# Four attention layers on one core: 64-row products issued together, feed-forward in fours, context values moved between passes

## The chip, the core and the metric

The kernel runs on one core of a Trainium2 chip. The core has a matrix engine (TensorE, PE in the profile, with weight loads listed apart as PEld), a vector engine (VectorE, DVE), an activation engine (ScalarE, ACT), a general engine (GpSimd, POOL) and SyncE (SP), which here only issues transfers. TensorE writes to PSUM, which has eight banks of 512 float32 values in each of 128 partitions. The metric is the device time of one execution in microseconds; of several runs the median counts.

## What is computed

The input x has 8 batches of 256 tokens with 320 channels, the context 8 batches of 120 tokens with 192 channels. Four layers follow each other:

```python
# layer 0: quantised attention, 20 heads of 16
def attention(x, ctx, Wq, Wk, Wv, Wo, bo, heads):
    q, k, v = fq_sym(x @ Wq), fq_sym(ctx @ Wk), fq_sym(ctx @ Wv)   # 8 bits, one step for the whole tensor
    ...
    w = fq_zero(softmax(q @ k * dh ** -0.5))                       # again one step for the whole tensor
    return (w @ v) @ Wo + bo
x = x + attention(layer_norm(x), layer_norm(x), ...)
x = x + attention(layer_norm(x), ctx, ...)
x = x + geglu_ff(layer_norm(x))        # (h @ W1 + b1) in halves a, g; a * gelu(g) @ W2 + b2; 320 -> 2 x 1280 -> 320
# layer 1: the same three steps without quantisation, exact gelu
# layer 2: attention to 104 text tokens plus attention to 16 image tokens, one output projection
# layer 3: attention to 116 tokens, 8 heads of 40, and a second chain of two small attentions with 4 tokens
```

A quantisation step needs the maximum over a whole tensor. So each attention of layer 0 is done in two passes: one to find the largest weight, one to compute with it.

## The kernel before

**Products of 320 rows.** A matrix product on TensorE contracts over partitions, at most 128. 320 channels are 128 + 128 + 64 rows, and the 192 channels of the context 128 + 64. The last 64 rows are kept twice, in the lower and in the upper half of the partitions. Two outputs are computed side by side: `duo` (L122) issues the 128-row terms of both, then the 64-row term of one output in the lower half of the array and that of the other in the upper half. `by_weight` and `by_token` (L132, L138) choose the halves. In the profile the 128-row terms are L127 and the 64-row terms L129. Each float32 product is two matmul records.

**PSUM.** `pair` gives two adjoining banks out of a rotation of three (6 banks, tile `pf`), `bank` a single one out of two (tile `pa`). A tile comes free when the engine that empties it is done.

**Layer 0's self attention** is an object `Quant`, called `s`; cross attention is another, `c`. `project_all` (L1143) runs over the batches: values, then the next batch's transposes (`turn`), then queries, keys, and the third 128 columns of both. In the first pass scores and their maxima (L1332, L1335), exponentials (L1376, L1383) and sums (L1398) are woven together. `weight_steps` (L1424) ends it: the logarithm of all sums on ScalarE (L1428), the smallest sum through a transpose and back (`all_max`, L469), the step (L1441), its logarithm (L1442). The second pass `out_all` (L1457) starts with `shift` (L1446), five VectorE steps on the logarithms, whose result `nTs` enters the scores through L1376.

**Between them** stands work for cross attention. `keys_all` is woven into s's first pass, `queries_all` (L1204) into its second: normalising on GpSimd (L301), transposes (L314) three rounds later, projections from the sixth. `values_all` (L1193) makes the context's values, one batch a step: four records of TensorE (L120, `pf<-v,ctxT`), a ScalarE copy (L1200), a VectorE maximum (L1139). Three steps are woven into the end of s's second pass and five into c's first pass.

**Keys and values of later layers** (`context_steps`, L642) are woven into c's two passes and go to DRAM; their 128-row products are L668, the 64-row ones L670.

**Feed-forward** (`ff_item`, L545) works on 512 tokens at a time, four items a layer. For each of 10 blocks of 128 hidden channels it takes a pair, issues four 128-row products (L564: gate and value, two terms each), two 64-row products (L568), GELU on ScalarE (L572) and a multiply on VectorE (L573), and yields. Then come 40 products with the second weight (L120).

**Order.** `weave` runs several generators in turn, and `run_flow` (L609) does so for the items of layers 1 to 3: while one item is in its main part, the next finds its score maxima, the one after it projects, and the one before finishes its output projection. Inside the order so written, a scheduler of the framework places the instructions of each engine[...].

Of the kernel before, what the change touches and what calls it, by code (L numbers as in the profile page):

```python
# [18 lines left out]
P = 128  # L19
# [35 lines left out]
class Kernel:  # L55
# [66 lines left out]
    def duo(self, outs, terms):  # L122

        n = len(terms[0]) - 1
        for c in range(n):
            for o, t in zip(outs, terms):
                self.nc.tensor.matmul(o, *t[c], start=c == 0, stop=False)  # L127
        for o, t in zip(outs, terms):
            self.nc.tensor.matmul(o, *t[n], start=False, stop=True)  # L129
# [176 lines left out]
    def turned(self, x, dst, at, ln=None):  # L306


        nc = self.nc
        ps = self.pair()  # L310
        for i, n in CH:
            for t in range(TPB):
                o = i % 2 * N + t * P
                nc.tensor.transpose(ps[:n, i // 2, o : o + P], x[:, t, i * P : i * P + n], self.ident)  # L314
        if ln is None:
            nc.scalar.copy(dst[:, :2, at : at + N], ps[:, 0, :].rearrange("p (c n) -> p c n", c=2))
            for r in (0, 64):
                nc.scalar.copy(dst[r : r + 64, 2, at : at + N], ps[:64, 1, :N])
            return
        for i, r, n in ((0, 0, P), (1, 0, P), (2, 0, 64), (2, 64, 64)):  # L320
            g = COL_LN + 6 * ln + i
            nc.scalar.activation(
                dst[r : r + n, i, at : at + N], ps[:n, i // 2, i % 2 * N : (i % 2 + 1) * N], AF.Identity,
                bias=self.cols[r : r + n, g + 3 : g + 4], scale=self.cols[r : r + n, g : g + 1],
            )
# [156 lines left out]
    def heads_item(self, b, ln, w, brow, kind):  # L482
# [4 lines left out]
        def project():  # L487
# [30 lines left out]
            self.duo([ps[:, m, :N] for m in range(2)], two((w["q"], w["q"]), (0, 1), 2))  # L518
            yield
            self.duo([ps[:, 0, N:]], two((w["q"],), (2,), 1))  # L520
# [24 lines left out]
    def ff_item(self, blk, ln, which, func, w, brow):  # L545
# [11 lines left out]
        def out():  # L557
            xT = it["x"]
            hT = [self.hp.tile([P, 4, 512], F32, tag="big", name="hT", bufs=4) for _ in range(3)]
            for i in range(NF):  # L560
                s = self.pair()
                for k, col in ((1, (NF + i) * P), (0, i * P)):
                    for c in range(2):
                        nc.tensor.matmul(s[:, k, :], w1[:, c, col : col + P], xT[:, c, :], start=c == 0, stop=False)  # L564

                for k in (1, 0):
                    r = 64 * k
                    nc.tensor.matmul(  # L568
                        s[:, k, :], w1c[r : r + 64, i * P : (i + 1) * P], xT[r : r + 64, 2, :], start=False, stop=True
                    )  # L570
                gl = self.work.tile([P, TB], F32, tag="gl", name="gl")
                nc.scalar.activation(gl, s[:, 1, :], func, bias=self.cols[:, b1 + NF + i : b1 + NF + i + 1])  # L572
                nc.vector.scalar_tensor_tensor(  # L573
                    hT[i // 4][:, i % 4, :], s[:, 0, :], self.cols[:, b1 + i : b1 + i + 1], gl, ALU.add, ALU.mult
                )
                yield
# [65 lines left out]
    def context_steps(self):  # L642
# [22 lines left out]
        def both(outs, whole, halves):  # L665

            for i, o in enumerate(outs):
                nc.tensor.matmul(o, *whole[i], start=True, stop=False)  # L668
            for i, o in enumerate(outs):
                nc.tensor.matmul(o, *halves[i], start=False, stop=True)  # L670

        def keys_to(ps, w, cols, b, k0, k1):
# [3 lines left out]
            for o, gs in cols:  # L676
# [4 lines left out]
                    [(w[half(i), 1, s], self.ctxT[half(i), 1, b, k0:k1]) for i, s in enumerate(c)],  # L681
# [196 lines left out]
    def last_item(self, b, w, brow, to):  # L878
# [8 lines left out]
        def project():  # L887
# [31 lines left out]
            for r in range(2):  # L919
                self.duo(  # L920
                    [ps[:, i, r * N : (r + 1) * N] for i in range(2)],
                    [self.by_weight(w["wq"], xT, 2 * r + i, i) for i in range(2)],
                )
# [7 lines left out]
            for c, t in ((0, 0), (1, 0), (0, 1), (1, 1), (2, 0), (2, 1)):  # L931
# [4 lines left out]
                    bd[rows, c, :nh, :].rearrange("p h r -> p (h r)"), start=c == 0, stop=c == 2,  # L936
# [180 lines left out]
class Quant:  # L1117
# [25 lines left out]
    def project_all(self):  # L1143
# [4 lines left out]
        def turn(b):  # L1148
            xT = k.work.tile([P, 3, N], F32, tag="xT", name="xT")
            k.turned(x, xT, 0, self.ln)  # L1150
# [4 lines left out]
        for b in range(B):  # L1155
# [6 lines left out]
            ps = k.pair()  # L1162
            k.duo([ps[:, t, :C] for t in range(TPB)], [k.by_token(w["v"], xT, t, t) for t in range(TPB)])
            nc.scalar.copy(v, ps[:, :, :C])
            if b + 1 < B:
                after = turn(b + 1)
            qv, kv = (a.rearrange("p (c n) -> p c n", c=3) for a in (q, kt))
            pq, pk = k.pair(), k.pair()
            for ps, n in ((pq, "q"), (pk, "k")):
                k.duo([ps[:, m, :N] for m in range(2)], [k.by_weight(w[n], xT, m, m) for m in range(2)])  # L1170
            k.duo([pq[:, 0, N:], pk[:, 1, N:]], [k.by_weight(w[n], xT, 2, i) for i, n in enumerate("qk")])
# [32 lines left out]
    def queries_all(self):  # L1204
# [20 lines left out]
        for r in range(5 * B + 4):  # L1225
            for b in range(B):
                if r - 5 * b in todo:
                    todo[r - 5 * b](b)
# [300 lines left out]
def kernel(ctx: ExitStack, tc: tile.TileContext, a, out):  # L1529
    k = Kernel(ctx, tc, a, out)  # L1530
    with ExitStack() as es:
# [15 lines left out]
        with tc.tile_pool(name="l0", bufs=1) as pool:  # L1547
            k.open_quant(pool)
            with tc.tile_pool(name="l0_keys", bufs=1, side="right") as kpool:
# [9 lines left out]
                for b in range(B):  # L1559
                    c.top(1, b, c.kk[b])  # L1560
                s.weight_steps()
                v = c.values_all()
                k.weave((0, s.out_all()), (8, c.queries_all()), (5 * B + 4, islice(v, 3)))
# [9 lines left out]
            for _ in c.whole(0, True):  # L1573
# [3 lines left out]
                (0, c.tops_all()), (n + 4, c.sums_all()), (0, c.whole_all()), (5, v),  # L1577
# [122 lines left out]
```

## Time and profile before

| | |
|---|---|
| runs | 2265.03, 2272.55, 2274.88 us; median 2272.55 |
| profiled execution | 2260.05 us |
| its span | 2258.2 us |
| granted TensorE clock, mean | 0.971 |
| TensorE busy | 2078.1 us (92%) |
| VectorE, ScalarE, GpSimd busy | 1119.0, 824.4, 363.2 us |
| layer 0: projections; self attention; cross attention | 13 to 112; 118 to 417; 424 to 678 us |
| layer 0 feed-forward; layer 1 attention; its feed-forward | 678 to 988; 989 to 1470; 1470 to 1750 us |
| layers 2 and 3 | from 1750 us |

The span goes from the first to the last instruction of the profiled execution. A row of a group names line, engine, operation, output and inputs and, behind an x, the number of records. Ends of matmul records are modelled, so starts are the surer quantity. The granted clock is the share of full speed that TensorE was allowed in a stretch.

### The profile page before, as it was taken

The numbers are of one execution on the slowest core, as the hardware profiler recorded it, in microseconds if no ns is written. First come the engines' busy times: TensorE is split into PE (matmuls) and PEld (weight loads), VectorE is DVE, ScalarE is ACT, GpSimd is POOL, SyncE is SP. The second block draws the span as 40 slices with busy tenths as digits, with TensorE's granted clock in tenths as the row PEclk, the third lists the DMA queues.
The fourth block names the chain that finished last, engine by engine and source line by source line (L and its number), as shares of the span: only waits on it lengthen the run. The fifth ranks groups of instructions, "written<-read, shape, count | busy, mean of one in ns | idle before, by whom it ended". The sixth has DMA issues, their size and how long they took to land.

```text
span 2258.2 us, 38244 instructions
## 1 busy us (share of the span) xinstructions
PE 2078.1 (92%) x16413; PEld 1177.0 (52%) x16413; DVE 1119.0 (50%) x1693; ACT 824.4 (37%) x1249; POOL 363.2 (16%) x368
## 2 busy tenths in 40 slices
PE   7978888898889999999999999899999799999997
PEld 4643345544444455465555555444455455566664
DVE  4288677444861221235555566611121566556465
ACT  2337878467542121124444443401201333222221
POOL 1093056620520000000000001100000100000100
PEclk9979889899899999999999999999999899999999
DMA  4010000542120000020000010100000201000000
GB/s 115 10 18 2 2 1 2 149 119 61 49 88 3 1 0 1 1 91 2 2 2 21 27 35 24 47 0 0 1 1 1 68 25 33 11 24 24 23 16 19
DMA packets 79304, 63.23 MB, mean 28 GB/s; under 512 B 48410, under 2 KB 68318, under 8 KB 78622
## 3 DMA queue, kind: packets, MB, share of 16 engines
q1 hardware_dynamic: 75070, 57.06, 9.0%
q10 hardware_dynamic: 4064, 3.71, 0.6%
q8 instruction: 130, 2.13, 0.4%
q14 instruction: 40, 0.33, 0.0%
HBM read 42.61 MB, written 17.37 MB: 27 GB/s over the span
## 4 chain that ended last, share of the span: by engine, by line
PE 74%; DVE 15%; ACT 4%; issue 2%; SPq 2%; DMA 1%; POOL 1%; ACTq 0%; DVEq 0%; POOLq 0%
PE pf L564 13%; PE pf L120 12%; PE pf L127 9%; PE pa L120 6%; PE pa L431 6%; PE pf L414 4%; PE pf L568 4%; PE pf L129 3%; DVE negm L1335 3%; PE pf L1376 3%; DVE rs L439 2%; PE pf L369 2%; PE pa L1398 2%; DVE negm L376 2%; DVE rs L1054 2%
## 5 line engine op out<-in xcount | busy, mean ns | idle before, releaser
L564 PE MATMUL pf<-xTf,ff 128*128 128x512 f32 x640 | 294.8, 603 | 3.5 <-DVE negm L376 2.5
L420 ACT ACTIVATE e<-pf 128x1024 f32<-128x1024 f32 (+2 forms) x176 | 157.7, 944 | 223.6 <-PE pf L414 216.8
L376 DVE TENSOR_REDUCE negm<-pf 128x4 f32<-128x1024 f32 (+4 forms) x224 | 187.8, 885 | 93.2 <-PE pf L369 93.2
L439 DVE RECIPROCAL rs<-pa 128x256 f32<-128x256 f32 x88 | 152.3, 1746 | 147.3 <-PE pa L431 147.3
L573 DVE SCALAR_TENSOR_TENSOR hT<-pf,cols_sb,gl 128x512 f32<-128x512 f32 x80 | 60.0, 750 | 331.2 <-ACT gl L572 331.2
L564 PEld LDWEIGHTS pf<-xTf,ff 128*128 128x128 f32 x640 | 115.1, 190 | 161.6 <-issue 154.9
L461 POOL TENSOR_TENSOR xb<-x_sb,brow 128x640 f32<-128x640 f32 x40 | 62.2, 1554 | 797.5 <-DVE x_sb L467 754.1
L1383 ACT ACTIVATE e<-pf,sc_s 128x1024 f32<-128x1024 f32 x160 | 169.6, 1117 | 50.8 <-PE pf L1376 44.7
L1335 DVE TENSOR_REDUCE negm<-pf 128x4 f32<-128x1024 f32 (+2 forms) x128 | 143.4, 1139 | 70.0 <-PE pf L1332 63.3
L120 PE MATMUL pf<-ff,hT 128*128 128x320 f32 x640 | 174.4, 434 | 0.0
L572 ACT ACTIVATE gl<-pf,cols_sb 128x512 f32<-128x512 f32 x80 | 55.0, 687 | 304.9 <-PE pf L568 304.9
L120 PEld LDWEIGHTS pf<-ff,hT 128*128 128x128 f32 x640 | 120.9, 190 | 55.5 <-issue 6.1
L414 PE MATMUL pf<-qT,kT 32*128 32x256 f32 (+1 forms) x1280 | 128.3, 411 | 19.3 <-DMA qT<-nT 11.0
L369 PE MATMUL pf<-kT,qT 32*128 32x120 f32 (+1 forms) x1920 | 112.7, 328 | 18.3 <-ACT e L420 18.3
L120 PE MATMUL pa<-o,oT 128*128 128x320 f32 x352 | 105.7, 442 | 12.8 <-DVE oT L440 11.6
L581 POOL TENSOR_TENSOR xb<-x_sb,brow 128x640 f32<-128x640 f32 x16 | 25.2, 1573 | 559.5 <-DVE x_sb L586 543.6
L369 PEld LDWEIGHTS pf<-kT,qT 32*128 32x128 f32 x1920 | 83.4, 189 | 55.4 <-ACT e L420 28.4
L1376 PE MATMUL pf<-Q,K 32*128 32x256 bf16 (+1 forms) x960 | 89.3, 294 | 24.9 <-DVE negm L1335 14.6
L431 PE MATMUL pa<-e,v 128*32 128x256 f32 (+1 forms) x1280 | 106.4, 389 | 2.3 <-ACT e L420 1.7
L414 PEld LDWEIGHTS pf<-qT,kT 32*128 32x128 f32 (+1 forms) x1280 | 72.2, 182 | 66.9 <-issue 34.6
L1491 DVE TENSOR_SCALAR w<-e 128x1024 bf16<-128x1024 f32 (+2 forms) x128 | 87.4, 691 | 37.4 <-ACT e L1383 36.4
L127 PE MATMUL pf<-xT,q 128*128 128x256 f32 x384 | 101.9, 394 | 2.1 <-DVE hT L573 1.9
(279 smaller groups left out, 3357.0 us busy)
## 6 DMA issues: line engine op xcount, KB each, us to landing
ff<-in_L_xattn_Wff_dram SPq DMA_DIRECT2D x1, 2560.0 KB
qT<-nT SPq DMA_DIRECT2D x160, 4.0 KB
ff<-in_L_xattn_ff_w_dram SPq DMA_DIRECT2D x1, 2560.0 KB
out_dram<-x_sb SPq DMA_DIRECT2D x16, 160.0 KB
kd_cross<-kst SPq DMA_DIRECT2D x8, 300.0 KB
vd_cross<-vst SPq DMA_DIRECT2D x8, 300.0 KB
vd_both<-vst SPq DMA_DIRECT2D x8, 300.0 KB
kT<-kd_cross SPq DMA_DIRECT2D x8, 300.0 KB
```

The costliest lines, as they stand in the source:

```text
L120: self.nc.tensor.matmul(out, l, r, start=i == 0, stop=i == len(pairs) - 1)
L127: self.nc.tensor.matmul(o, *t[c], start=c == 0, stop=False)
L369: nc.tensor.matmul(s[j // 2][:, j % 2, o : o + nk], qT[r : r + PAD, g, t * P : (t + 1) * P], kT[r : r + PAD, g, :nk], start=True, stop=True,)
L376: nc.vector.tensor_reduce(negm[:, n, 2 * i : 2 * i + 2, g0 : g0 + len(gs), :].rearrange("p j g t -> p j (g t)"), sv[:, :, :, k0:k1], AX.X, ...
L414: nc.tensor.matmul(s[j // 2][:ks, j % 2, o : o + N], kT[r : r + PAD, g, c * ks : (c + 1) * ks], qT[r : r + PAD, g, :], start=True, stop=True,)
L420: nc.scalar.activation(e[:ks, 2 * i : 2 * i + 2, :n], s[i][:ks, :, :n], AF.Exp, scale=scale)
L431: nc.tensor.matmul(o[j * PAD : (j + 1) * PAD, what * N : (what + 1) * N], w, es[g][:ks, j, c * N : (c + 1) * N], start=first and c == 0 an ...
L439: nc.vector.reciprocal(rs, o[:, N:])
L564: nc.tensor.matmul(s[:, k, :], w1[:, c, col : col + P], xT[:, c, :], start=c == 0, stop=False)
L1335: nc.vector.tensor_reduce(negm[:, 2 * h : 2 * h + 2, gs[0] : gs[-1] + 1, :].rearrange("p j g t -> p j (g t)"), s[:, :, : len(gs) * TPB * n ...
L1376: nc.tensor.matmul(s[at // 2][:ks, at % 2, o : o + N], l, m, start=not shift and o == 0, stop=shift and o + N == n, skip_group_check=True,)
L1383: nc.scalar.activation(e[:ks, :, :n], ps[:ks, :, :n], AF.Exp, scale=self.sc[:ks, 9:10])
```

## The change

There are four edits, and nothing that is computed changes.

1. Where a function had several 64-row stretches close to each other, they are issued together. `duo` is split into `whole_rows` and `half_rows`; a sum may now begin with its 64-row term (`start` with the halves) and end with its 128-row terms. This touches `project_all`, the query projection of cross and of both attention, the context keys, and the last layer's projections.
2. Feed-forward works through blocks in fours: two blocks' 128-row products, then the 64-row products of these two and of the next two, then the 128-row products of the next two. Two blocks of four use pairs as before, the third a pair, the fourth the two single banks. A manual dependency keeps the row forms in this order.
3. `turned` can put its transposes in two single banks, which `project_all` now uses, as its three pairs are held over the transposes.
4. Cross attention's context values: two steps before s's `weight_steps`, three in the first rounds of s's second pass, three at its end as before; none is left in c's first pass. The first batch's transposes in `queries_all` come in round 4 instead of 3.

```diff
     def duo(self, outs, terms):
+        self.whole_rows(outs, terms, True, False)
+        self.half_rows(outs, terms, False, True)
+
+    def whole_rows(self, outs, terms, start, stop):
         n = len(terms[0]) - 1
         for c in range(n):
             for o, t in zip(outs, terms):
-                self.nc.tensor.matmul(o, *t[c], start=c == 0, stop=False)
+                self.nc.tensor.matmul(
+                    o, *t[c], start=start and c == 0, stop=stop and c == n - 1, skip_group_check=True
+                )
+
+    def half_rows(self, outs, terms, start, stop):
         for o, t in zip(outs, terms):
-            self.nc.tensor.matmul(o, *t[n], start=False, stop=True)
+            self.nc.tensor.matmul(o, *t[-1], start=start, stop=stop, skip_group_check=True)
...
-    def turned(self, x, dst, at, ln=None):
+    def turned(self, x, dst, at, ln=None, singles=False):
-        ps = self.pair()
+        if singles:
+            ps = [self.bank(), self.bank()]
+        else:
+            pair = self.pair()
+            ps = [pair[:, 0, :], pair[:, 1, :]]
...
             ps = self.pair()
-            self.duo([ps[:, m, :N] for m in range(2)], two((w["q"], w["q"]), (0, 1), 2))
-            yield
-            self.duo([ps[:, 0, N:]], two((w["q"],), (2,), 1))
+            outs, terms = [ps[:, m, :N] for m in range(2)], two((w["q"], w["q"]), (0, 1), 2)
+            last = [ps[:, 0, N:]], two((w["q"],), (2,), 1)
+            self.duo(outs, terms)
+            self.half_rows(*last, False, False)
+            yield
+            self.whole_rows(*last, False, True)
...
+            for i in range(0, NF, 4):
+                for j in range(i, min(i + 2, NF)):
+                    ps = self.pair()
+                    s[j] = ps[:, 0, :], ps[:, 1, :]
+                    whole(j, True)
+                    yield
+                for j in range(i, min(i + 2, NF)):
+                    halves(j, False)
+                    gated(j)
+                if i + 2 < NF:
+                    ps = self.pair()
+                    s[i + 2] = ps[:, 0, :], ps[:, 1, :]
+                    s[i + 3] = self.bank(), self.bank()
+                    for j in (i + 2, i + 3):
+                        halves(j, True)
+                    for j in (i + 2, i + 3):
+                        whole(j, False)
+                        gated(j)
+                        yield
...
             ps = self.pair()
-            for r in range(2):
-                self.duo(
-                    [ps[:, i, r * N : (r + 1) * N] for i in range(2)],
-                    [self.by_weight(w["wq"], xT, 2 * r + i, i) for i in range(2)],
-                )
+            self.duo(*sums[0])
+            self.half_rows(*sums[1], False, False)
+            self.whole_rows(*sums[1], False, True)
...
-            for c, t in ((0, 0), (1, 0), (0, 1), (1, 1), (2, 0), (2, 1)):
+            for c, t in ((2, 0), (2, 1), (0, 0), (1, 0), (0, 1), (1, 1)):
...
+            k.duo(*values)
+            for i in range(2):
+                k.half_rows(*qk[i], True, False)
+            k.half_rows(*last, False, False)
+            nc.scalar.copy(v, pv[:, :, :C])
             if b + 1 < B:
                 after = turn(b + 1)
+            for i in range(2):
+                k.whole_rows(*qk[i], False, True)
+            k.whole_rows(*last, False, True)
...
-                if r - 5 * b in todo:
-                    todo[r - 5 * b](b)
+                n = r - 5 * b - (b == 0 and r in (3, 4))
+                if n in todo:
+                    todo[n](b)
...
+                v = c.values_all()
+                for _ in islice(v, 2):
+                    pass
                 s.weight_steps()
-                v = c.values_all()
-                k.weave((0, s.out_all()), (8, c.queries_all()), (5 * B + 4, islice(v, 3)))
+                k.weave((0, s.out_all()), (8, c.queries_all()), (0, islice(v, 3)), (5 * B + 4, v))
...
-                (0, c.tops_all()), (n + 4, c.sums_all()), (0, c.whole_all()), (5, v),
+                (0, c.tops_all()), (n + 4, c.sums_all()), (0, c.whole_all()),
```

`whole(j, first)`, `halves(j, first)` and `gated(j)` are the four 128-row products, the two 64-row products, and GELU with multiply of block j. In `context_steps`, the second product of each key computation likewise begins with its 64-row terms.

## The prediction

> **What bounds the kernel now.** I first read the page's engine totals and the chain that ended last: TensorE is busy 92% of the span and carries 74% of the chain, VectorE 15%.
>
> ```profile
> PE 2078.1 (92%) x16413; PEld 1177.0 (52%) x16413; DVE 1119.0 (50%) x1693; ACT 824.4 (37%) x1249; POOL 363.2 (16%) x368
> PE 74%; DVE 15%; ACT 4%; issue 2%; SPq 2%; DMA 1%; POOL 1%; ACTq 0%; DVEq 0%; POOLq 0%
> ```
>
> A share over the whole span hides stages with different limits, so next I read busy time by stretch (us, then busy PE, weight load, DVE, ACT, POOL, granted clock, DMA share, GB/s). The stretches are layer 0's projections, the two feed-forwards, layer 1's attention, the last layer, cross attention's first pass, and the start of self attention's second pass.
>
> ```profile
> 13.00:112.00 99.00, 94.17 (x432) 62.20 (x432) 28.73 (x56) 36.02 (x73) 5.98 (x10) 1.00 0.14 32
> 678.00:988.00 310.00, 306.12 (x1025) 152.38 (x1024) 68.20 (x118) 55.80 (x96) 18.79 (x21) 1.00 0.04 12
> 1470.00:1750.00 280.00, 278.01 (x958) 138.13 (x957) 43.72 (x63) 40.20 (x68) 12.04 (x8) 1.00 0.00 1
> 895.00:1215.00 320.00, 307.63 (x2637) 178.72 (x2639) 153.21 (x181) 111.13 (x166) 18.43 (x17) 0.99 0.06 19
> 1910.00:2180.00 270.00, 256.20 (x2254) 167.45 (x2254) 146.88 (x180) 71.66 (x114) 20.32 (x31) 1.00 0.07 23
> 428.00:557.00 129.00, 119.73 (x1181) 62.08 (x1182) 60.02 (x100) 80.85 (x159) 37.40 (x31) 0.92 0.37 96
> 267.00:300.00 33.00, 25.59 (x273) 12.41 (x273) 31.66 (x78) 25.78 (x26) 3.94 (x3) 0.66 0.00 1
> ```
>
> The first three are TensorE-bound at full clock: what TensorE no longer does there leaves the span one for one. In the next three it is at 93 to 96% and part of a saving turns into waits. In the last it isn't the limit.
>
> A busy TensorE need not be multiplying. In the timeline I therefore compared starts (columns: start, us of the group, engine, line, operation; each float32 product is two records).
>
> ```profile
> 831.34 3.70 PE L564 MATMUL pf<-xTf,ff 128*128 128x512 f32 x8
> 834.97 1.13 PE L568 MATMUL pf<-xTf,ff1c 64*128 64x512 f32 x4
> 836.03 1.99 PE L127 MATMUL pf<-xT,k 128*128 128x256 f32 x8
> 837.95 0.70 PE L129 MATMUL pf<-xT,k 64*128 64x256 f32 x4
> 838.58 0.70 PE L564 MATMUL pf<-xTf,ff 128*128 128x512 f32 x1
> ...
> 2000.25 1.12 PE L1017 MATMUL pf<-qT,kz 64*116 64x256 f32 x8
> 2001.30 0.53 PE L1034 MATMUL pa<-ef,v 128*32 128x192 f32 x8
> ```
>
> Weight loads inside a run of L564 start 0.43 us apart, so a 512-column record costs 0.43 and a 256-column one 0.215; two 64-row records (upper and lower half of the array) run side by side. From start to start: L564 takes 3.63 for 8 x 0.43 = 3.44; L568 1.06 for 2 x 0.43 = 0.86; L127 1.92 for 1.72; L129 0.63 for 0.43. **Every run exceeds its streaming time by 0.19 to 0.20 us, whatever its length**: entering another row form costs 0.20. L1017 is the proof that this is per run: four pairs in a row take 1.05 for 4 x 0.215 = 0.86, again 0.19 over. A visit to 64 rows from 128 and back costs 0.40.
>
> Here the Trainium skill bears (TensorEngine Tiling (Array Packing), Key Properties): a change of tiling mode, not of tile, drains the array. It names no price. TensorE: Matmul & The Clock Gate, Single matmul latency, gives some 166 ns as the fixed part of an isolated warm product; were that the price, the 208 changes below would be worth 34.5 us, against 41.6 by the rows. I use the rows.
>
> **The change part by part.** I counted changes of form (rows x columns of the array) in the order in which the two programs issue to TensorE; the 64-column transposes don't count, since they follow at the unchanged 109 ns. 1608 becomes 1400, 208 fewer at 0.20.
>
> *Projections of layer 0*: four visits per batch become one; 63 changes become 16. 47 x 0.20 = 9.4 us, the stage TensorE-bound. The transposes now use the two single banks, since three pairs are held; their four activations (2.04 us) fit under the twelve 128-row products behind them (5.2 us). One new wait: in the first batch the 64-row rows of k are needed at about 23 us instead of 28, while SP issues k's last weights from 21.20 to 23.43. Behind it on TensorE stand the next transposes and so ScalarE. Bounds 0 and 5 us (unhindered at 28.7 before); I take 1.5, nearer the end of issue. Net 7.9.
>
> *Feed-forward*: an item has 10 visits and keeps 3. With what is woven in, the two stages go from 103 and 93 changes to 49 and 37: 110 x 0.20 = 22.0. The cost is PSUM. Two pairs are open at the first yields, then one pair and both single banks, eight banks at the fullest. The Trainium skill speaks against this (the same page, Gotcha 1: PSUM Pressure): row tiling raises PSUM pressure. In the trace, emptying a pair after its last product takes 1.6 us (836.03 to the product's end 837.62: GELU 0.69, multiply 0.75, gaps). In the order a bank is asked for again mostly after two 128-row groups (6.9 us), so that is covered. It isn't in item 3 of each layer, where the next attention's maxima (1.22 us a reduction) and projections want pairs too: three or four of their waits are on a reduction or GELU just issued, up to 1 us each. Zero to 4 us per such item; I take 2 each, by the 1.9 us that L564 already waits for a reduction there. Net 18.
>
> *Context keys and values of later layers* (L668, L670): 16 changes fewer, 3.2, some at half clock; TensorE 93% busy: 2. *Query rows of cross and both attention*: 14 fewer, 2.8, I take 2. *Last layer*: 24 fewer, 4.8 at 95%: 3.5.
>
> *Context values moved.* Five of the eight leave cross attention's first pass. Each is four records, one ScalarE copy (0.43), one reduction (0.49), and no DMA, so no queue of SP or POOL moves. Start to start they take 2.28 (half clock) and four times 1.1 to 1.2, 6.9 in all; the chain lists L120 with 4.7% of 135 us, 6.3. I take 5. They come back here:
>
> ```profile
> 266.48 1.91 ACT L1428 ACTIVATE sums<-sums 128x2048 f32<-128x2048 f32 x1
> 267.46 0.15 DVE L1441 TENSOR_SCALAR sc_s<-most 128x1 f32<-128x1 f32 x1
> 268.29 0.19 ACT L1442 ACTIVATE sc_s<-sc_s 128x1 f32<-128x1 f32 x1
> 271.33 1.03 PE L1376 MATMUL pf<-nTs,sel 32*128 32x256 bf16 x12 [4.10 <-DVE nTs L1455]
> ...
> PE pf L314 <- POOL xh L301: 4.9, 2, 2.8
> ```
>
> TensorE stands from 267.2 to 271.3, so the products themselves are free. Not so the rest: in the new order the two copies stand behind the long logarithm, their two reductions ahead of L1441 on VectorE, and L1442 waits for that. Copies from 268.4, reductions to 269.9, L1442 at 270.2 instead of 268.3: 1.9 late, plus a third reduction of 0.49 inside the shift's chain: **+2.4**. Two more copies in the next rounds, where ScalarE is full: +0.9. Three more changes of form: +0.6. The first transposes of cross attention's queries move one round later; TensorE waits 4.9 us there for GpSimd's normalising, and a round (about 2 us) now goes ahead of it: -2. Sum of this part -5 + 2.4 + 0.9 + 0.6 - 2 = -3.1.
>
> The half clock from 267 to 300 may end sooner when the hole is partly filled. ScalarE is full at the same time, so I count nothing; cover gone, only the output projection at 286.9 (3.5 us at half clock) gains 1.8.
>
> Sum: 7.9 + 18 + 2 + 2 + 3.5 + 3.1 = **36.5 us**. The profiled execution took 2260.05 (span 2258.2 and 1.9 around it), so 2223.5 for one like it. The median of the three runs is 2272.55, 12.5 above that execution; with the same distance 2236.
>
> **The rivals.**
>
> *Only the saturated stages pay.* Outside projections and feed-forward TensorE waits for softmax steps in turn, and the moved values cancel: 14 to 27 us, say 2251. For: VectorE's 15% of the chain. Against: 26 of the 36.5 lie where TensorE is 95% busy and more.
>
> *All of it pays*, the first wait is zero and pairs are never short: 36.5 + 1.5 + 4 + 4 = 46, 2226. The order makes pairs short in two items, so less likely.
>
> *PSUM becomes the bound, and it gets slower.* At each of the 24 groups of 64-row products TensorE would wait until both pairs ahead are emptied, 1.6 + 0.75 = 2.4 us: 58 us against 36.5, 2294. It decides from 1.5 us a group. Against it: the order reuses banks 6.9 us later.
>
> *Nothing happens*, because the drain comes with each pair: 2272. The L1017 row excludes it for 256 columns; for 512 it isn't shown.
>
> **How the numbers follow.** The forecast 0.68 (28 to 46 saved), only the saturated stages 0.22, more than 46 0.04, nothing 0.02, PSUM 0.04. Half a per cent, 11 us, is about what a measurement tells from no change. Faster by more: 0.68 + 0.04 + most of 0.22 = 0.93; within 0.03; slower 0.04. The range must leave no more than 2 in 10: 2220 (52 saved, all bounds favourable plus the spread of runs, 5 us) to 2256 (16 saved).
>
> **What would show it.** After: feed-forward groups of eight 64-row products at about 3.6 us and 128-row runs of 16 products; a feed-forward stretch about 9 us shorter per layer; a projection stretch of about 91 us; the same 0.20 at each change left; L1513 (was L1442) 2 us later; no L120 on ctxT in the first cross pass. I am wrong if L582 waits on the multiply at each group, if the 64-row chain takes more than 0.86 us per product pair, or if the stretch from 895 to 1215 grows by what feed-forward loses.

## The result

| | before | after |
|---|---|---|
| median | 2270.28 us (4 runs, 2265.03 to 2274.88) | 2237.3 us (4 runs, 2226.97 to 2240.71) |
| profiled execution, its span | 2260.05, 2258.2 us | 2240.71, 2238.6 us |
| mean granted TensorE clock in it | 0.971 | 0.961 |

The ratio is 0.9848, with a 95% interval of 0.9808 to 0.9888: the change makes the kernel faster by 25 to 44 us, 33 by the medians. Repeated on another occasion in five runs it gave 2240.64 us and a ratio of 0.9877 (0.9853 to 0.9901); over all nine runs of it the median is 2237.4 us.

The two profiled executions are an uneven pair: that of before lies 10 us under its median, that of after 3 us over. The granted clock goes with it. Of two runs of the changed kernel the one at 2226.97 us had a mean clock of 0.967, the one at 2240.71 us 0.961: 0.006 of 2237 us would be 13.4 us, if TensorE set the pace throughout, of the 13.7 between them. Over 39 runs of the kernel before, taken with the first experiments, a line through times and clocks gives 1.9 us for each 0.001. So I compare stages only where the clock is the same, and say so where it isn't.

First the page of after, engine totals and the chain that ended last:

```profile
PE 2057.3 (92%) x16413; PEld 1206.2 (54%) x16413; DVE 1121.2 (50%) x1693; ACT 823.1 (37%) x1249; POOL 363.3 (16%) x368
PE 75%; DVE 16%; ACT 5%; issue 3%; DMA 1%; POOL 0%; SPq 0%; ACTq 0%; DVEq 0%; POOLq 0%
```

TensorE has as many records as before (16413) and is busy 20.8 us less; no other engine's work changed by more than 3 us (weight loads, which lie under the products, read 29 us more). That is what fewer changes of row form look like: the same products, less between them, and here at a lower mean clock, which stretches the products.

Then busy time by stretch of after, in the same order and with the same columns as in the prediction (stretch, us, busy PE, weight load, DVE, ACT, POOL, granted clock, DMA share, GB/s):

```profile
13.00:103.00 90.00, 85.29 (x432) 66.20 (x432) 31.13 (x57) 36.01 (x73) 6.32 (x10) 1.00 0.15 37
676.00:977.00 301.00, 296.64 (x1023) 157.47 (x1020) 68.35 (x118) 55.38 (x96) 18.65 (x21) 1.00 0.04 12
1447.00:1734.00 287.00, 284.29 (x990) 151.51 (x992) 51.96 (x79) 47.08 (x79) 13.36 (x10) 1.00 0.01 2
883.00:1197.00 314.00, 301.38 (x2569) 177.54 (x2568) 150.02 (x178) 108.26 (x161) 17.99 (x16) 0.99 0.06 18
1894.00:2160.00 266.00, 252.51 (x2269) 170.28 (x2268) 147.33 (x182) 72.36 (x114) 20.30 (x31) 1.00 0.07 23
417.00:551.00 134.00, 122.03 (x1176) 63.52 (x1170) 60.86 (x98) 79.89 (x154) 40.55 (x33) 0.85 0.38 97
263.00:296.00 33.00, 26.84 (x286) 12.97 (x286) 31.28 (x74) 24.70 (x25) 4.81 (x3) 0.74 0.00 1
```

The projections fill 90 us in place of 99, the first feed-forward 301 in place of 310. The rows of the second one can't be compared, 287 against 280: before, it began at 1452.98 us and not at 1470, and from its first product to its last it takes 286.00 us in place of 295.36 (shown below). The last two rows are the ones to stop at. Cross attention's first pass, with five values fewer in it, is not shorter (134.51 us whole, 133.49 before), and its clock is 0.85 where it was 0.92. The start of self attention's second pass has the better clock, 0.74; before, the 33 us from the first product with `nTs` at 271.33 had 0.60 (the prediction's row, at 0.66, begins in the standstill).

The timeline of after shows the new order inside a feed-forward item, the run that still begins a visit, and the first batch of the projections (start, us, engine, line, operation, records):

```profile
17.65 4.63 PE L132 MATMUL pf<-v,xT 128*128 128x320 f32 x8 [2.12 <-ACT xT L336]
22.21 1.13 PE L139 MATMUL pf<-v,xT 64*128 64x320 f32 x4
23.18 0.59 PE L139 MATMUL pf<-xT,q 64*128 64x256 f32 x4
23.62 0.59 PE L139 MATMUL pf<-xT,k 64*128 64x256 f32 x4
...
843.06 3.70 PE L582 MATMUL pf<-xTf,ff 128*128 128x512 f32 x8
846.69 2.85 PE L582 MATMUL pf<-xTf,ff1c 64*128 64x512 f32 x12
849.37 1.02 PE L582 MATMUL pa<-xTf,ff1c 64*128 64x512 f32 x4
850.33 1.98 PE L582 MATMUL pf<-xTf,ff 128*128 128x512 f32 x4
```

Eight 64-row products (16 records) take 850.33 - 846.69 = 3.64 us from start to start, 8 x 0.43 + 0.20, as forecast. The eight 128-row records ahead of them take 3.63, again 0.19 over 3.44. And k's 64-row terms start at 23.62 with no wait noted. Here SP issued k's last weights from 19.91 to 22.14 us, 1.3 us sooner than in the profile from which I had the bound.

### The profile page after: what moved, and what is told of

Read it like the earlier page. It is cut to its first block, busy times and chain, and to the rows that moved or that the text cites. A ratio compares the mean times of both kernels' runs of the same rounds, so it can differ in the third digit from the quotient of the medians.

```text
span 2238.6 us, 38248 instructions
## 1 busy us (share of the span) xinstructions
PE 2057.3 (92%) x16413; PEld 1206.2 (54%) x16413; DVE 1121.2 (50%) x1693; ACT 823.1 (37%) x1249; POOL 363.3 (16%) x368
## 4 chain that ended last, share of the span: by engine, by line
PE 75%; DVE 16%; ACT 5%; issue 3%; DMA 1%; POOL 0%; SPq 0%; ACTq 0%; DVEq 0%; POOLq 0%
PE pf L582 13%; PE pf L120 13%; PE pf L132 9%; PE pa L120 7%; PE pa L445 6%; PE pf L428 4%; PE pa L582 3%; PE pf L726 3%; PE pf L383 3%; PE pf L139 3%; DVE negm L1406 3%; DVE rs L453 2%; PE pf L1447 2%; PE pa L1469 2%; DVE negm L390 2%
## 5 line engine op out<-in xcount | busy, mean ns | idle before, releaser
L390 DVE TENSOR_REDUCE negm<-pf 128x4 f32<-128x1024 f32 (+4 forms) x224 | 188.1, 886 | 113.6 <-PE pf L383 113.6
L582 PE MATMUL pf<-xTf,ff 128*128 128x512 f32 x512 | 230.8, 597 | 5.4 <-DVE negm L390 5.2
L609 DVE SCALAR_TENSOR_TENSOR hT<-pf,cols_sb,gl 128x512 f32<-128x512 f32 x64 | 48.0, 751 | 256.4 <-ACT gl L608 254.1
L582 PEld LDWEIGHTS pf<-xTf,ff 128*128 128x128 f32 x512 | 94.3, 190 | 124.6 <-issue 118.5
L608 ACT ACTIVATE gl<-pf,cols_sb 128x512 f32<-128x512 f32 x64 | 43.9, 687 | 248.0 <-PE pf L582 248.0
L1562 DVE TENSOR_SCALAR w<-e 128x1024 bf16<-128x1024 f32 (+2 forms) x128 | 89.2, 706 | 35.4 <-ACT e L1454 34.2
```

The lines of the kernel that those rows point to most:

```text
L390: nc.vector.tensor_reduce(negm[:, n, 2 * i : 2 * i + 2, g0 : g0 + len(gs), :].rearrange("p j g t -> p j (g t)"), sv[:, :, :, k0:k1], AX.X, ...
L582: ins = nc.tensor.matmul(*args, **kw)
```

## The experiments

The theory: a change of row form costs 0.20 us wherever TensorE sets the pace. The rivals: the savings turn into waits outside projections and feed-forward; or the parts don't add up. And one question from the profile: why did cross attention's first pass gain nothing?

### The parts alone

Four kernels make one part of the change each, on the kernel before. First, feed-forward in fours:

```diff
+            for i in range(0, NF, 4):
+                for j in range(i, min(i + 2, NF)):
...
+                    whole(j, True)
...
+                    for j in (i + 2, i + 3):
+                        halves(j, True)
...
```

> Only the feed-forward's products in fours; everything else as before. 110 changes of row form fewer. Theory (0.20 us a change, TensorE the limit there): the stretch from the first feed-forward product to the last one of an item's second half is 9 to 10 us shorter in each of the two layers, the whole 18 to 22 us shorter, about 2250. Rival (the pairs of PSUM run short, TensorE waits on the multiply at each group): less than 10 us saved, with L582's successor waiting on VectorE.

Measured: 2252.22 us against 2268.4, ratio 0.9928 (0.9904 to 0.9952), 16 us saved (11 to 22). By stretch, from the first product with the first weight to the last with the second, before:

```profile
678.74:988.36 309.62, 305.74 (x1019) 152.12 (x1020) 67.58 (x118) 55.18 (x95) 18.05 (x21) 1.00 0.04 12
1452.98:1748.34 295.36, 293.37 (x975) 144.92 (x974) 51.10 (x77) 46.90 (x79) 13.11 (x9) 1.00 0.01 2
```

and with feed-forward in fours alone:

```profile
685.10:985.28 300.18, 296.07 (x1020) 157.47 (x1020) 68.08 (x118) 54.96 (x95) 18.07 (x21) 1.00 0.04 12
1454.69:1741.49 286.80, 284.08 (x975) 150.34 (x974) 51.47 (x77) 47.11 (x79) 13.14 (x9) 1.00 0.01 2
```

9.44 and 8.56 us, at full clock. The pure price is 54 and 56 changes at 0.20: 10.8 and 11.2. So 1.4 and 2.6 us a layer come back, which I had put at 2. In the changed kernel the same stretches are 9.43 and 9.36 us shorter; the second holds four changes of the attention's query rows as well, and the small edits alone shorten it by 0.79. PSUM is not the bound: in the changed kernel's two stretches TensorE waits before L582 for 3.4 and 2.7 us in all, 0.7 of it for a multiply, where it waited 2.4 and 1.1 us before L564. Most of it is waiting for a reduction of the next attention's maxima (L390), as forecast.

Second, the projections:

```diff
+            k.duo(*values)
+            for i in range(2):
+                k.half_rows(*qk[i], True, False)
+            k.half_rows(*last, False, False)
...
+            for i in range(2):
+                k.whole_rows(*qk[i], False, True)
+            k.whole_rows(*last, False, True)
```

> Only layer 0's projections with one visit to 64 rows per batch, and the transposes through the two single banks. 47 changes of row form fewer. Theory: the first stage ends 9.4 us sooner if the 64-row rows of k are there in time, 7.9 if TensorE waits 1.5 us for them; the whole 8 to 9.5 us shorter, about 2261. Rival (what is taken from the projections turns into waits of the steps behind them): under 4 us.

Measured: 2261.09 against 2268.4, ratio 0.9965 (0.9945 to 0.9986), 3 to 12 us. From the first product to the maxima's transposes the stage takes 90.42 us, 9.2 less than 99.60. TensorE doesn't wait for k's weights here either.

Third, the moved values:

```diff
+                v = c.values_all()
+                for _ in islice(v, 2):
+                    pass
                 s.weight_steps()
-                v = c.values_all()
-                k.weave((0, s.out_all()), (8, c.queries_all()), (5 * B + 4, islice(v, 3)))
+                k.weave((0, s.out_all()), (8, c.queries_all()), (0, islice(v, 3)), (5 * B + 4, v))
...
-                (0, c.tops_all()), (n + 4, c.sums_all()), (0, c.whole_all()), (5, v),
+                (0, c.tops_all()), (n + 4, c.sums_all()), (0, c.whole_all()),
```

> Only cross attention's values moved between the passes of self attention, with batch 0's transposes one round later. Forecast: 3 us shorter in all: first pass of cross attention 7 us shorter, start of self attention's second pass 2.4 us later, 1.5 us more in its rounds. Rival (the first pass of cross attention does not become shorter, because its first rounds lie at half clock and take 5.5 to 6.5 us each with the values or without): 0 to 5 us longer in all, and its first pass shorter by less than 2 us.

Measured: 2273.84 against 2268.4, ratio 1.0004 (0.9982 to 1.0025): nothing gained, though by this run alone up to 4 us saved isn't excluded. The first pass takes 138.10 us where it took 133.49, at a clock of 0.82 in place of 0.91. The rival's reading is the one that fits, and it went further than the rival put it.

Fourth, the three small edits, of which this is the last layer's:

```diff
-            for r in range(2):
-                self.duo(
...
+            self.duo(*sums[0])
+            self.half_rows(*sums[1], False, False)
+            self.whole_rows(*sums[1], False, True)
```

> Only the three small edits: the context's keys and values of later layers with 64-row terms first in every second group, the query rows of cross and both attention, and the last layer's queries. 54 changes of row form fewer. Forecast: 7.5 us shorter (2 + 2 + 3.5), about 2262. Rival (in these stages TensorE waits for softmax steps in turn, so what it saves becomes a wait): 0 to 3 us.

Measured: 2256.12 against 2268.4, ratio 0.9952 (0.9932 to 0.9972), 11 us saved by the ratio (6 to 15). 54 changes at 0.20 are 10.8. So here it pays too, though TensorE is busy only 93 to 96% of these stages, and the rival that only saturated stages pay falls. Whether all of it pays this run can't tell, as its interval holds my 7.5 as well. The profiles lean to the whole price: from the end of the second feed-forward to the end, five profiles without these edits take 511.4 us on the mean and seven with them (and no other change there) 504.5. That is 6.8 us for 30 changes, 6.0 by the price.

By their ratios the four parts come to 16.3 + 7.9 + 10.9 - 0.9 = 34 us, and the whole change to 34.5: they add up, within intervals of about 5 us for each part.

### The price of a visit

```diff
                 for k, col in ((1, (NF + i) * P), (0, i * P)):
                     for c in range(2):
+                        if (k, c) == (0, 1):
+                            halves(0, 256, False)
                         nc.tensor.matmul(s[:, k, :], ...)
-                for k in (1, 0):
...
+                halves(256, 512, True)
```

> The kernel before with the feed-forward's 64-row terms in two visits of 256 columns instead of one of 512: 80 visits more, the same columns streamed. Theory (0.40 us a visit, whatever its length, TensorE the limit): 32 us slower, about 2300, each feed-forward stretch 16 us longer. At 0.166 us a change: 26.6. Rival (the drain lies under the products of the other form): 0 to 10 us.

Measured: 2304.82 against 2267.5, ratio 1.0173 (1.013 to 1.0216), 29 to 49 us slower. The two stretches:

```profile
681.47:1008.87 327.40, 323.53 (x1180) 161.25 (x1180) 67.61 (x118) 55.20 (x95) 18.08 (x21) 0.99 0.03 11
1478.28:1789.77 311.49, 309.49 (x1136) 153.63 (x1134) 51.12 (x77) 46.90 (x79) 13.13 (x9) 1.00 0.01 2
```

The second, at full clock, is 16.13 us longer for 40 visits: 0.403 us a visit, 0.20 a change, for products of 256 columns put between products of 512. At 0.166 it would have been 13.3. The first is 17.78 longer, part of it at half clock. The price is shown; that nothing happens for 512 columns is excluded.

### Why the moved values gained nothing

The changed kernel with the values back where they were (the diff of the third part, reversed):

> The changed kernel with cross attention's values and batch 0's transposes back where they were before; all other parts of the change stay. The forecast held the moved values for worth 3 us: then this is 3 us slower than the changed kernel, about 2240. The reading of the runs so far (the move makes the half clock at the start of cross attention's first pass last 34 to 48 us instead of 17, which takes back all it gains): 0 to 5 us faster than the changed kernel, 2232 to 2237, with a half clock of 17 to 21 us there and of about 34 us at the start of self attention's second pass.

Measured: 2233.62 us (2226.66 to 2241.99), ratio 0.9854 (0.9815 to 0.9892). Once more, side by side with the changed kernel itself:

> The changed kernel once more, beside the same without the moved values: 2237 as before, with a half clock of 30 us or more at the start of cross attention's first pass if that is a property of the order of work, and a different length if it is chance.

> The changed kernel without the moved values once more. By the forecast 3 us slower than the changed kernel; by the runs so far 0 to 4 us faster, 2233 to 2237. The half clock at the start of cross attention's first pass: 20 us or less if that is a property of the order of work.

Measured: 2240.64 us with the moved values (0.9877, 0.9853 to 0.9901) and 2231.78 without (0.9849, 0.9824 to 0.9873). Over nine runs of each the means are 2237.2 and 2232.5: **the move costs 4.7 us, give or take 4.7** (95%, from the spread of the runs), where I had it save 3.1. So it saves nothing; how much it costs is less sure.

What the clock has to do with it was asked by two kernels. One fills the standstill ahead of the pass:

```diff
+    def filler(self, n, width=448):
+        ps = self.bank()
+        rhs = self.ctxT[:, 0].rearrange("p b m -> p (b m)")[:, :width]
+        for _ in range(n):
+            self.nc.tensor.matmul(ps[:, :width], self.ident, rhs, start=True, stop=True)
...
             c.steps()
+            k.filler(5)
```

> The changed kernel with five products of 448 columns more, whose sums nobody reads, in the 4 us in which TensorE stands between the maxima and the first score of cross attention's first pass. If the half clock there follows from that standstill: no half clock from 414 to 448, the pass 12 to 17 us shorter, in all about 2223. If it follows from what the first rounds hold: the window stays at 17 us or more, and the time at 2237.

Measured: 2225.25 us (2214.28 to 2227.69), ratio 0.9806 (0.9768 to 0.9844), the pass 124.57 us in place of 134.51. Busy time around the standstill in the changed kernel (columns as above):

```profile
412.00:417.00 5.00, 0.71 (x17) 0.50 (x17) 3.64 (x12) 2.12 (x6) 3.56 (x4) 0.84 0.71 193
417.00:432.00 15.00, 13.03 (x60) 7.67 (x56) 7.18 (x11) 4.76 (x12) 15.00 (x13) 0.50 0.43 139
432.00:447.00 15.00, 12.84 (x70) 6.18 (x69) 4.98 (x6) 4.14 (x16) 15.00 (x14) 0.53 0.52 130
```

in the kernel before, whose pass starts 8 us later:

```profile
420.00:425.00 5.00, 0.85 (x18) 0.59 (x18) 3.52 (x12) 1.90 (x6) 3.70 (x4) 0.91 0.67 191
425.00:440.00 15.00, 13.04 (x51) 6.87 (x52) 6.78 (x9) 4.77 (x12) 15.00 (x13) 0.50 0.28 98
440.00:455.00 15.00, 14.39 (x92) 8.22 (x91) 8.48 (x14) 6.33 (x23) 15.00 (x14) 0.96 0.62 159
```

and with the standstill filled:

```profile
413.00:417.00 4.00, 4.00 (x13) 1.84 (x14) 3.29 (x10) 1.57 (x5) 3.12 (x4) 1.00 0.68 203
417.00:432.00 15.00, 11.88 (x111) 7.06 (x111) 9.59 (x14) 7.07 (x18) 15.00 (x13) 1.00 0.70 183
432.00:447.00 15.00, 11.63 (x92) 6.24 (x91) 9.97 (x11) 7.69 (x24) 15.00 (x13) 0.87 0.58 173
```

Both kernels stand about 4 us and come out at half clock. Then they part: the kernel before reaches full clock in its second 15 us, the changed one stays down. With the standstill filled the clock holds through the first 15 us and falls later, at 443.09, for 6.8 us. The pass is 9.9 us shorter, where 12 to 17 were expected.

Busy time doesn't tell what holds or lifts the clock: at 11.88 of 15 us it held, at 11.63 it fell, and at 13.04 it stayed down. The trace has every switch of the clock on record. In all fourteen profiles each stretch at half clock inside the span is a whole number of steps of 3.41 us. Four such steps of the kernel before (the standstill, one at half clock, the last at half clock, the first at full), then the same four of the changed one (columns as above):

```profile
420.65:424.06 3.41, 0.00 (x0) 0.00 (x0) 2.95 (x10) 1.25 (x4) 2.76 (x4) 1.00 0.67 215
427.47:430.89 3.42, 3.24 (x24) 1.35 (x20) 0.17 (x1) 0.63 (x2) 3.42 (x4) 0.50 0.14 40
437.72:441.13 3.41, 2.87 (x6) 1.98 (x7) 3.14 (x7) 2.29 (x7) 3.41 (x4) 0.50 0.41 162
441.13:444.54 3.41, 3.41 (x23) 1.91 (x22) 1.05 (x2) 0.92 (x3) 3.41 (x4) 1.00 0.05 18
412.03:415.44 3.41, 0.22 (x1) 0.13 (x1) 2.60 (x11) 2.09 (x6) 2.00 (x3) 1.00 0.72 196
418.85:422.27 3.42, 3.42 (x25) 2.01 (x24) 0.50 (x1) 0.17 (x1) 3.42 (x3) 0.50 0.41 119
442.75:446.16 3.41, 3.41 (x8) 1.50 (x8) 1.16 (x1) 0.00 (x0) 3.41 (x4) 0.50 0.58 179
446.16:449.58 3.42, 2.36 (x28) 1.52 (x27) 2.46 (x5) 2.61 (x8) 3.42 (x4) 1.00 0.37 99
```

A step that is busy throughout (from 418.85) leaves the clock at half; one that is busy 2.87 of 3.41 us (from 437.72) ends it. What tells them apart is how much of the array the products fill. An estimate from the records' sizes: each counts with its streaming time (0.43 us for 512 columns of float32 at full clock, twice that at half, and half as long in bf16, the 16-bit type of the scores), times its rows and columns of the array as shares of 128. By that the step from 437.72 is filled to 0.76, and this is where the first of the values' products stand:

```profile
438.26 2.49 PE L120 MATMUL pf<-v,ctxT 128*120 128x320 f32 x4 [0.74 <-DVE negm L1335]
```

The step from 418.85, with 64-row pairs, changes of form and 32-row scores in it, comes to 0.69. Over all fourteen profiles, from 25 to 2150 us, 203 of 209 steps at half clock with a fill of 0.75 and more ended it, and 2 of 276 with less than 0.65. At full clock, none of 7762 steps with 0.40 and more was followed by half clock, and 208 of 229 with less than 0.34 were.

The other kernel puts five products of the values' shape back into rounds 5 to 9, without copies and maxima:

```diff
+    def fillers_all(self, n):
+        k, w = self.k, self.w
+        for b in range(n):
+            ps = k.pair()
+            k.mm(ps[:M, 0, :C], [(k.ctxT[:, c, b, :], w["v"][:, c, :]) for c in range(2)])
+            yield
...
-                (0, c.tops_all()), (n + 4, c.sums_all()), (0, c.whole_all()),
+                (0, c.tops_all()), (n + 4, c.sums_all()), (0, c.whole_all()), (5, c.fillers_all(5)),
```

> The changed kernel with five products of the values' shape, whose sums nobody reads, in rounds 5 to 9 of cross attention's first pass, where the values stood before; neither copies nor maxima with them. If these products ended the half clock there: it lasts 17 to 21 us again, and with 5 us more of products the pass is not longer (0 to 3 us shorter), about 2236. If the half clock lasts for another reason: 34 us or more of it, the pass 5 us longer, about 2242.

Measured: 2234.27 us (2225.31 to 2238.81), ratio 0.9862 (0.9826 to 0.9897), the pass 128.85 us. With more work in it than the changed kernel's, the pass is 5.7 us shorter, and the half clock behind the standstill lasts 20.5 us, as expected if these products end it.

All profiles of this pass in one table. The half clock of the whole pass is worked out from its granted clock: length x (1 - clock) x 2. The last column is the one stretch at half clock right behind the standstill, from the clock's record; it begins up to 2 us ahead of the pass.

| kernel | values in the pass | length, us | clock | at half clock, us | stretch behind the standstill, us |
|---|---|---|---|---|---|
| before | yes | 133.49 | 0.91 | 24 | 17.1 |
| feed-forward in fours alone | yes | 133.74 | 0.91 | 24 | 17.1 |
| projections alone | yes | 135.37 | 0.90 | 27 | 20.5 |
| small edits alone | yes | 134.18 | 0.88 | 32 | 17.1 |
| more visits | yes | 133.01 | 0.91 | 24 | 17.1 |
| changed, values back | yes | 126.64 | 0.97 | 8 | 3.4 |
| the same once more | yes | 134.28 | 0.88 | 32 | 17.1 |
| changed | no | 134.51 | 0.85 | 40 | 30.7 |
| changed, once more | no | 134.20 | 0.84 | 43 | 37.5 |
| values moved alone | no | 138.10 | 0.82 | 50 | 47.8 |
| changed, products in rounds 5 to 9 | products only | 128.85 | 0.93 | 18 | 20.5 |
| changed, standstill filled | no | 124.57 | 0.95 | 12 | none |
| four standstills filled | no | 122.57 | 0.96 | 10 | none |
| the same and a fifth, values back | yes | 126.48 | 0.97 | 8 | none |

Behind an unfilled standstill the clock stays at half for 30.7 us and more in every pass without the values, and for 20.5 or less in every pass with them or with their bare products. In seven of these eight it rises at the end of the step in which the first of those products start, or of the next. In the eighth (3.4 us) the first step behind the standstill was already full enough. So the products that were moved away are those that ended the half clock. The length is partly chance: one and the same order had 3.4 and 17.1 us (17 to 21 were expected), another 30.7 and 37.5. The steps fall differently against the work: in the profile with 3.4 us a step began 0.08 us ahead of the first score, in the one with 17.1 it was 0.92.

Among the passes without the values the length grows by (138.10 - 122.57)/(50 - 10) = 0.39 us per us of half clock. The changed kernel's 40 us against 24 before thus cost 16 x 0.39 = 6 us. At equal half clock (the last two rows) the values are worth 3.9 us, near the 5 of the forecast.

### More standstills filled

```diff
                 s.steps()
+                k.filler(5)
...
             c.weight_steps()
+            k.filler(3)
...
-        k.run_flow(items, before, {3: load_ff1, 12: load_ff1_row, 23: load_last})
+        k.run_flow(items, before, {3: load_ff1, 12: load_ff1_row, 23: load_last, 24: lambda: k.filler(12)})
```

> The changed kernel with products whose sums nobody reads in four standstills: five after layer 0's self attention maxima, five after cross attention's (as in the run before), three after cross attention's sums, twelve ahead of the last layer, where TensorE stands 12 us for a transfer. If a half clock follows a standstill: the windows of 17 us at 102 and at 1752 go, 10 to 16 us less than with one standstill filled, about 2212. Rival (the half clock at those places follows from the thin work of the rounds behind, or the filler pushes back what waits behind it): 2225 or more.

> As the run before, but with cross attention's values and batch 0's transposes where the kernel before had them, and five filler products in the standstill between self attention's passes in their place. With the half clock out of the way the moved values can be judged by their products, copies and maxima alone: by the forecast (5 us out of the first pass against 4 put in) this is up to 3 us slower than the run before; if the values' products lay in slack of the first pass it is the same or up to 4 us faster.

Measured: 2226.58 us (2224.57 to 2234.55; ratio 0.9835, 0.981 to 0.986), and with the values back 2222.44 (2218.43 to 2230.5; 0.9815, 0.9788 to 0.9842). The mean clock of the profiled execution rises to 0.976, but the time does not follow: my 2212 was wrong. In the first stage the filler itself runs into half clock and holds the first score back:

```profile
105.13 5.68 PE L127 MATMUL pa<-ctxT,ident 128*128 128x448 f32 x10
110.74 0.61 PE L1410 MATMUL pf<-K,Q 32*128 32x256 bf16 x12
```

5.68 us instead of the 4.03 of the same products ahead of cross attention. Counted from the product before it, the first score comes 1.8 us later than in the changed kernel. Which of the other fillers helped isn't shown: cross attention's second part, from the end of its first pass to the feed-forward, takes 120.8 and 120.2 us with a filler ahead of it and 120.5 to 128.6 in the kernels without one. Between the two kernels, the pass with the values is 3.9 us longer and self attention's second pass 1.0 us shorter; the rest of their 4 us lies in later stages that have the same code, and the intervals overlap. The fastest two, the changed kernel with one standstill filled and the last kernel, both beat before and after and can't be told apart.

## Why the prediction was right, and where not

The forecast was 2236 us with a range of 2220 to 2256; 2237.3 was measured. In what is saved the two are a little further apart: 36.5 us forecast, 33.0 measured by the medians and 34.5 by the ratio, as the median of before came out 2.3 us lower with a fourth run. Step by step:

- **Price of a change of form, 0.20 us.** Right, and now measured by itself: 0.403 us a visit. The lower price of 0.166 is out, by 16.13 against 13.3 us.
- **Projections, net 7.9.** 9.2 and 9.6 us in the profiles of the part alone and of the whole. The term that was mis-sized is "I take 1.5" for k's last weights: the wait is 0, as they were issued 1.3 us sooner.
- **Feed-forward, net 18.** 18.0 us in the profiles of the part alone (9.44 + 8.56), 11 to 22 by its runs. What comes back was put at 2 us a layer and is 1.4 and 2.6. (The page on PSUM pressure that the prediction means is TensorEngine Tiling (Array Packing).)
- **The three small edits, 2 + 2 + 3.5.** 11 us (6 to 15), and the full price is 10.8. The discount for stages at 93 to 96% looks too large, by the profiles of layers 2 and 3 too (6.8 us for a price of 6.0), but the interval doesn't exclude it.
- **Context values, -3.1.** This step failed: no saving, but +4.7, give or take 4.7. Two of its sub-steps were wrong. The main one: "The half clock from 267 to 300 may end sooner ... I count nothing" asked only about the place the products go to. There it was right: the stretches at half clock came to 24 us in place of 34, and the second pass was no shorter. At the place they leave, the pass has 16 us more of half clock in the changed kernel (40 against 24; right behind the standstill 30.7 against 17.1) and 20 on the mean of all unfilled passes (44 against 24); that is 6 to 8 us and takes back the 5. Behind it stands how the prediction read that pass: TensorE busy 93% at a clock of 0.92 was taken for work that can be removed, and not for products that bring the clock back. The other: "The first transposes ... move one round later ... -2". The wait for GpSimd's normalising did go, but waits for L1562's weights, L336's copies and exponentials came, and the second pass takes 148.4 us on the mean of six profiles with the move, 146.8 on the mean of eight without. Of the rest, +2.4 was nearly right. The chain in after:

```profile
256.44 1.91 ACT L1499 ACTIVATE sums<-sums 128x2048 f32<-128x2048 f32 x1
258.26 0.73 ACT L1270 COPY V<-pf 120x320 f32<-120x320 f32 x2
259.67 0.20 ACT L1513 ACTIVATE sc_s<-sc_s 128x1 f32<-128x1 f32 x1 [0.68 <-DVE sc_s L1512]
263.00 0.61 PE L1447 MATMUL pf<-nTs,sel 32*128 32x256 bf16 x12 [1.71 <-DVE nTs L1526]
```

From the logarithm's start to L1513 it is 3.23 us (1.81 before), to the first product with `nTs` 6.56 (4.85 before): +1.7. On the means of the profiles the unfilled first pass is 2.6 us longer without the values and the second 1.6 longer with the move; with the 1.7 that is 5.9, which fits the 4.7 of the runs.

So the hit is partly luck: 11 us from the small edits where I had 7.5, and 1.5 more in the projections, made good for 5 of the 8 us that the values missed. Of the rivals, "only the saturated stages pay" is refuted by the small edits, though it had the moved values right: they cancel. The others fall, "PSUM becomes the bound" by the waits before L582, "nothing happens" by the visits. "All of it pays" had the first wait right, and missed the pairs of PSUM and the values. The sign I gave for being wrong, layer 1's attention growing by what feed-forward loses, did not come: from the end of the first feed-forward to the start of the second, the profile of after has 470.6 us against 464.6. But the second profile of the same kernel has 464.8, and of four other kernels with before's code there three have 469.2 to 469.4, one 465.9. Before's profile lies at the low end of its own spread.

Here the Trainium skill bears (TensorE: Matmul & The Clock Gate, Part 1: The HAM clock gate). It says that TensorE falls to half clock after an idle window of some 3.4 us and is back after one such window of sustained activity. The steps of 3.41 us agree, and so does the fall: each half clock behind this standstill follows a step in which TensorE is busy 0 to 25%. Read as the profile's busy time, the second half would say that the moved values couldn't matter, since in the changed kernel the second step behind the standstill is busy throughout; yet the clock stayed at half for 30.7 us. Read as fill of the array it agrees: one step with 0.75 and more was enough in 203 of 209 cases. The runs don't show how the chip itself counts.

## What to carry to other kernels

Count the changes of row form in the order of issue and price each at what the shortest runs of the trace show over their streaming time; where TensorE is busy 93% and more, the whole price fits these runs better than a discount. When work is taken out of a stretch, ask whether TensorE has just stood still there: work that fills little of the array can stay at half clock behind a standstill, however busy TensorE looks, and the products removed may be the ones that ended it. Filling one such standstill with products whose sums nobody reads (5 of them, 4 us) was worth 10 us in the pass and 12 by the medians; moving real work into another one was worth nothing. Three more fillers brought nothing that the runs can tell.

## What the runs showed of the hardware

- A stretch at full clock repeats very exactly: the second feed-forward took 285.99 or 286.00 us in eight profiles. The spread between runs lies in other stages.
- A visit from 128-row to 64-row products and back costs 0.40 us: 40 visits more, of 256 columns, made a stretch at full clock 16.13 us longer. With 512 columns each of the two changes shows as 0.19 to 0.20 us (3.63 and 3.64 us for 3.44 of streaming).
- Half clock comes in steps of 3.41 us and outlasts its cause: behind one and the same standstill of 4 us it lasted from 3.4 to 47.8 us, depending on the products that follow.
- Busy time doesn't tell what the clock will do. The fill of the array (the estimate above) nearly does: steps over 0.75 ended half clock in 203 of 209 cases, and steps over 0.40 were never followed by it.
